# A perceiver of two layers on one core: averages 22 tiles behind the scores, weighing and spreading one step later, more one-step pauses, and the apart rows through W_k transposed

## The chip, the core and the metric

The kernel runs on one core of one Trainium2 chip. The metric is the device time of one execution in microseconds (us); smaller is better. A core has a matrix engine (TensorE, PE in the profile), a vector engine (VectorE, DVE), a scalar engine (ScalarE, ACT), a general engine (GpSimd, POOL) and a synchronising engine (SyncE, SP) that here issues most of the DMA transfers. Each runs its own stream of instructions in order; they wait for one another through semaphores.

## The reference, cut to what matters

Sixty-four latents of width 128 for each of 16 batches pass through two layers. Each layer has a cross attention over 1601 context tokens plus the latents themselves (16 heads of 64), a recurrent mixer and a feed-forward part, each behind a layer norm and with a residual:

```python
x = x + L0_xattn(ctx, layernorm(x), ...)      # 16 heads of 64, keys: 1601 context tokens and 64 latents
x = x + L0_attn(layernorm(x), ...)            # selective scan, 256 channels, 16 states
x = x + L0_ffn(layernorm(x), ...)             # small attention, then 8 experts of which 2, and a shared one
x = x + L1_xattn(ctx, layernorm(x), mask, ...)# the same attention with a mask on the context
x = x + L1_attn(layernorm(x), ...)            # convolution and scan with 4 heads of 64 by 64 states
x = x + L1_ffn(layernorm(x), ...)             # FP4-quantised gated feed-forward, 352 wide
...
logits = einsum('bhld,bhsd->bhls', q * scale, k * scale)
w = softmax(logits);  out = einsum('bhls,bhsd->bhld', w, v);  return out.reshape(B, L, INNER) @ Wo
```

All is float32.

## The kernel before

W_q and W_k are folded into one 128 by 128 matrix per head (`fold`, line 329), and W_v and W_o into another, so a head's scores are the normalised context times the folded queries, and keys and values are both just the normalised context. 1601 is not a multiple of 128: twelve tiles of 128 keys and a thirteenth that holds 64 more and the latents make 1600 + 64. The 1601st token of each batch is held **apart**: its scores `se` come from a product of its own (`apart_scores`), and its weight is `ee`.

The attention is 64 groups (layer, batch, half of the heads), each of NT = 13 key tiles, so 832 steps. A group's rows are 8 heads times 64 latents, 512 columns. `run` (line 1425) counts steps n, and `step` (1569) writes down what step n holds:

- `scores` of tile i of group g: a product of 128x512 into one of three PSUM buffers (line 662; it shows as two records), a running maximum R over the tiles on DVE (670, 672), and an eviction into a score buffer st by ACT (675, 677). The st buffers hold pairs of tiles; there are 12 of them.
- `average` (715) of the tile LAG = 21 steps earlier: st as the weights, the context tile as the moving side, into two PSUM buffers (line 725, four products, eight records a step). At the last tile `gather` (727) adds the apart token's share and makes aq.
- Of a group p whose scores are over, o = steps since: at o = 1 `maximum` (680): four transposes of R (tm), a reduction on DVE over them (692), the maximum with se, and ee; at o = 3 `spread` (700): four transposes that spread the maximum over all rows, mb, which stays in PSUM; at odd o from 3 `weigh` (707), one pair of tiles at a time: DVE subtracts mb (712), ACT takes the exponential (713). The averages of the group follow.
- Of a group whose averages are over: at o = 1 the reciprocal of the denominators, at o = 5 `turn` (776: four transposes `at`, and an ACT copy into aT, 786), at o = 8 of each second batch `output` (791).

Beside this go generators. Those in `prep` make a batch ready: `fold_qk` and `fold_vo`, `apart` (362), `latents`, `queries`, `context` (582: the loaded context's mean, line 613, variance, normalisation, and transposes kt and kt_r into kvT), `apart_scores`. Each live one is advanced by one yield a step. Those in `between` are the rest of the layers: `setup_rest`, `scan0` and `moe` (916) for four groups of batches, `scan1` (1123) and `ffn` (1372) for five; a budget per step says how many yields they get. A generator that yields HOP1, HOP, HOP3 or HOP4, `(1,)` to `(4,)`, sleeps that many steps; it is put where an engine's result is to be ready before the next instruction asks for it.

All small products go through `tp` (93), a pool of three PSUM buffers. The scheduler that builds the program may move instructions, but `behind` (1552) keeps them from moving ahead of the score step they were written in. In layer 0 there are three context buffers kv; the load of batch b is issued 48 steps ahead on SP's queue and waits for the last average of batch b-3.

`apart` before: the normalised last tokens of the 16 batches are transposed (xet, line 386, then xeT). Then, for four heads at a time, the folded matrices are transposed (line 394), copied by ACT, and multiplied by xeT (399) to give `ge`, by which `apart_scores` multiplies each pair of batches' latents. Each layer has 16 transposes and 16 products of 16 columns.

Of the kernel before, what the change touches and what calls it, by code (L numbers as in the profile page):

```python
# [32 lines left out]
F32 = mybir.dt.float32  # L33
# [9 lines left out]
P = 128  # L43
NB, L, D = 16, 64, 128
# [6 lines left out]
H, DH = 16, 64  # L51
NEG = -1.0e30
NT = G + 1
NQ = 512
LAG = 21

(LN1W, LN1B, LN2W, LN2B, NORMW, NORMB, G1, G2, YG1, YB1, YG2, YB2) = range(12)
LNOFF = 12
# [6 lines left out]
HOP1, HOP, HOP3, HOP4 = (1,), (2,), (3,), (4,)  # L65
# [8 lines left out]
CG = 2  # L74
# [5 lines left out]
class Kernel:  # L80
# [248 lines left out]
    def fold(self, lay, dst, l, r, scale):  # L329


        nc = self.nc
        for g in range(H // 4):
            if (lay, l) == (0, "WqT"):
                raw = self.raw0[g]
            else:
                raw = self.raw_pair(lay, l, r, g, nc.sync)
            if lay == 0 and l == "WvT":
                yield HOP3
            ts = [self.tp(f"{l}{lay}{g}{i}") for i in range(2)]  # L340
            for m in range(2):
                for i in range(2):
                    half = slice(i * DH, (i + 1) * DH)
                    nc.tensor.matmul(ts[i][:, m * D:(m + 1) * D], raw[0][half, m, :], raw[1][half, m, :], start=True, stop=True)
            for i in range(2):
                to = dst[:, g * 4:g * 4 + 4, :].rearrange("p (m i) d -> p i m d", i=2)[:, i]
                t = ts[i][:, :2 * D].rearrange("p (m d) -> p m d", m=2)
                if (lay, l) == (0, "WqT") and g < 2:
                    nc.scalar.activation(to, t, AF.Copy, scale=scale)
                else:  # L350
                    nc.vector.tensor_scalar_mul(to, t, scale)
            yield 0.7

    def fold_qk(self, lay):
        self.wqk = self.at.tile([P, H, D], F32, tag="wqk", name=f"wqk{lay}")
        yield from self.fold(lay, self.wqk, "WqT", "WkT", 0.125)
        self.raw0 = None

    def fold_vo(self, lay):
        self.wvo = self.at.tile([P, H, D], F32, tag="wvo", name=f"wvo{lay}")  # L360
# [1 line left out]
    def apart(self, lay):  # L362

        nc = self.nc
        w1 = self.vecs_of(lay)[0]
        xe = self.xe
        if lay == 0:
            mean, rstd, v = (self.sm([NB, 1], f"e{x}") for x in ("mean", "rstd", "var"))
            scr = self.at.tile([NB, D], F32, tag="raw", name="escr", bufs=3)
            nc.vector.tensor_reduce(mean, xe, AX.X, ALU.add)  # L370
            nc.vector.tensor_scalar_mul(mean, mean, 1.0 / D)
            nc.vector.tensor_scalar(xe, xe, mean, None, ALU.subtract)
            nc.scalar.activation(scr, xe, AF.Square)
            yield HOP1
            nc.vector.tensor_reduce(v, scr, AX.X, ALU.add)
            nc.vector.tensor_scalar(v, v, 1.0 / D, 1e-5, ALU.mult, ALU.add)
            nc.gpsimd.tensor_tensor(rstd, v, self.neghalf[:NB, :1], ALU.pow)
            yield HOP1
            nc.vector.tensor_scalar(xe, xe, rstd, None, ALU.mult)
        xw = self.at.tile([NB, D + 1], F32, tag="raw", name=f"xw{lay}", bufs=3)  # L380
        nc.vector.memset(xw[:, D:], 1.0)
        nc.vector.tensor_tensor(xw[:, :D], xe, self.vec[:NB, w1, :], ALU.mult)
        nc.sync.dma_start(out=self.xed[lay], in_=xw)
        yield HOP
        t = self.tp(f"xet{lay}")
        nc.tensor.transpose(t[:, :NB], xw[:, :D], self.ident[:NB, :NB])
        self.xeT = self.at.tile([P, NB], F32, tag="xeT", name=f"xeT{lay}")
        nc.vector.tensor_copy(self.xeT, t[:, :NB])
        yield 0.7
        self.ge = self.at.tile([P, NB, H], F32, tag="ge", name=f"ge{lay}")  # L390
        for g in range(H // 4):
            t = self.tp(f"wkq{lay}_{g}")
            for k in range(4):
                nc.tensor.transpose(t[:, k * D:(k + 1) * D], self.wqk[:, g * 4 + k, :], self.ident)
            w = self.at.tile([P, 4, D], F32, tag="raw", name=f"wkq{lay}s{g}", bufs=3)
            nc.scalar.copy(w.rearrange("p h d -> p (h d)"), t)
            o = self.tp(f"ge{lay}_{g}")
            for k in range(4):
                nc.tensor.matmul(o[:, k * NB:(k + 1) * NB], w[:, k, :], self.xeT, start=True, stop=True)
            nc.vector.tensor_copy(self.ge[:, :, g * 4:g * 4 + 4], o[:, :4 * NB].rearrange("p (h b) -> p b h", h=4))  # L400
            yield 0.7

    def apart_scores(self, lay, c):

# [511 lines left out]
    def moe(self, gr):  # L916
        nc, tc, a = self.nc, self.tc, self.a
        X = self.X[:, gr * CG:(gr + 1) * CG, :]
        with tc.tile_pool(name="mo1", bufs=1) as one, tc.tile_pool(name="mo2", bufs=2) as work:
# [8 lines left out]
            xi, nx, xT = t1([P, CG, D], "xi"), t1([P, CG, D], "nx"), t1([P, TG], "xT")  # L928
            mv, (r, rr) = self.moments(X, CG, [LN, LNRMS])
            yield 0.8  # L930
            yield HOP1
            self.scaled(nc.vector, nx, X, mv, rr, CG)
            self.scaled(nc.gpsimd, xi, X, mv, r, CG)
            yield 0.8
# [5 lines left out]
            t = self.tp("mq")  # L940
            nc.tensor.matmul(t[:, :TG], fWqT, xT, start=True, stop=True)
            nc.scalar.copy(q, t[:, :TG])
            yield 0.4
            t = self.tp("mk")
            nc.tensor.matmul(t[:, :TG], fWk4.rearrange("p r n -> p (r n)"), xT, start=True, stop=True)
            nc.scalar.copy(kT, t[:, :TG])
            t = self.tp("mv")
            for c in range(CG):
                nc.tensor.matmul(t[:, c * 32:(c + 1) * 32], xT[:, c * P:(c + 1) * P], fWkvT[:, 32:], start=True, stop=True)
# [4 lines left out]
            n = 2 * BG  # L954
            shape = [P, n, L]
            sc = t1(shape, "sc")
            m = self.sm([P, n], "mm")

            ts = [self.tp(f"ms{i}") for i in range(2)]
# [4 lines left out]
            for i in range(2):  # L964
                t3, mi, half = ts[i][:, :TG].rearrange("p (n l) -> p n l", l=L), m[:, i * BG:(i + 1) * BG], [P, BG, L]
# [5 lines left out]
            d, r = self.sm([P, n], "md"), self.sm([P, n], "mr")  # L971
# [8 lines left out]
            for j in range(2):  # L980
                t = self.tp(f"mt{j}")
# [18 lines left out]
            o = self.tp("mo")  # L1000
# [30 lines left out]
            for e in range(NE + 1):  # L1031
                w = work.tile([P, 3, FF], F32, tag="ew", name=f"ew{e}", bufs=3)
                for x, i in enumerate((1, 3, 2)):
                    nc.sync.dma_start(out=w[:, x, :], in_=a[f"e{i}T"][e])
                gu = self.tp(f"gu{e}")
                nc.tensor.matmul(gu[:, :TG], w[:, 0, :], xT, start=True, stop=True)
                nc.tensor.matmul(gu[:, TG:], w[:, 1, :], xT, start=True, stop=True)
                sg, th = (work.tile([P, TG], F32, tag=x, name=f"{x}{e}") for x in ("sg", "th"))
                nc.scalar.activation(th, gu[:, :TG], AF.Tanh, scale=0.5)
                if last:  # L1040
                    second(*last)
                    yield 0.7
                yield HOP1
                nc.vector.scalar_tensor_tensor(sg, th, 1.0, gu[:, :TG], ALU.add, ALU.mult)
                nc.vector.scalar_tensor_tensor(sg, sg, 0.5, gu[:, TG:], ALU.mult, ALU.mult)
                yield 0.9
                last = e, w, sg
# [75 lines left out]
    def scan1(self, c0, CG):  # L1123
# [5 lines left out]
        with tc.tile_pool(name="sd1", bufs=1) as one, tc.tile_pool(name="sd2", bufs=CG) as work:  # L1129
# [128 lines left out]
            for c in range(CG):  # L1258
                tok = slice(c * P, (c + 1) * P)
                for i in range(2):  # L1260
                    g = self.tp(f"gr{c}{i}")
                    part = slice(i * HD, (i + 1) * HD)
                    for k in range(2):
                        nc.tensor.matmul(g[:, k * P:(k + 1) * P], bT[part, k, tok], cT[part, k, tok], start=True, stop=True)
                    gi = gm[c].rearrange("p (k i) t -> p i k t", i=2)[:, i]
                    nc.vector.tensor_tensor(gi, g[:, :2 * P].rearrange("p (k t) -> p k t", k=2), self.row(self.upto, [P, 2, P]), ALU.mult)
                yield 0.9
            for c in range(CG):
                for lo, hi in parts:
                    sg = self.tp(f"seg{c}")  # L1270
                    for h in range(lo, hi):
                        mm = nc.tensor.matmul(sg[:, h * P:(h + 1) * P], af[c][:, h, :], self.upto, start=True, stop=True)  # L1272
                    if last and hi == NH:
                        self.fill(2, mm)
                    decay = nc.scalar.activation(af[c][:, lo:hi, :].rearrange("p h t -> p (h t)"), sg[:, lo * P:hi * P], AF.Exp)
                yield 0.1
# [292 lines left out]
    def step(self, n, ng):  # L1569
# [25 lines left out]
        for p in (g - 2, g - 1):  # L1595
            o = n - (p + 1) * NT
            if not 0 <= p < ng:
                continue
            if o == 1:
                with self.behind():  # L1600
                    self.maximum(p)
            elif o == 3:
                with self.behind():
                    self.groups[p]["mb"] = self.spread(self.groups[p]["m"], f"mb{p}")
            if o > 2 and o % 2 and (o - 3) // 2 < (NT + 1) // 2:
                self.weigh(p, (o - 3) // 2)

        d, o = divmod(n - LAG - NT, NT)
        if 0 <= d < ng:
# [69 lines left out]
```

## Time and profile before

| | us |
|---|---|
| median of 3 runs | 1976.11 |
| lowest, highest | 1975.02, 1976.44 |
| the profiled execution | 1976.84 |
| its span, first to last instruction | 1975.1 |

A profile is one execution seen by the hardware profiler. Its page gives each engine's busy time, the span in 40 slices, and the costliest groups of instructions: line, engine, operation, output and inputs, shape and count, then busy time and the mean of one in ns, then the idle time of that engine just before them and whose result ended it. A matrix product in float32 is two records. The mean granted clock of TensorE is 0.999 of full speed. A few more groups of the page:

```profile
L713 ACT ACTIVATE st<-st 128x1024 f32<-128x1024 f32 (+1 forms) x448 | 444.4, 996 | 121.6 <-DVE st L712 114.8
L712 DVE TENSOR_TENSOR st<-st,mb 128x1024 f32<-128x1024 f32 (+1 forms) x448 | 503.5, 1134 | 17.9 <-PE mb L704 17.8
L675 ACT ACTIVATE st<-s,mcol 128x512 f32<-128x512 f32 x416 | 283.4, 684 | 191.4 <-DVE R L670 167.2
L677 ACT COPY st<-s 128x512 f32<-128x512 f32 x416 | 240.0, 580 | 127.7 <-DVE R L672 117.2
```

The pair subtraction (1134 ns) and the exponential that waits for it (996 ns) come every other step; the two lines below are the eviction of the scores in the second and the first layer, which comes after the running maximum of the same tile.

### The profile page before, as it was taken

What the parts mean: (1) busy time and instruction counts of PE and PEld (TensorE: products, weight loads), DVE (VectorE), ACT (ScalarE), POOL (GpSimd) and SP (SyncE); (2) the same over time, 40 slices, a digit from 0 to 9 for tenths busy, and PEclk for the clock granted to TensorE, in tenths of its full rate; (3) what the DMA queues carried; (4) which work ended last, traced back from release to release, by engine and by line L of the source; (5) the groups of instructions that cost most, each with busy time, mean ns of one, the idle gap of its engine ahead of it and who ended that gap; (6) DMA issues with size and microseconds to landing.
All of it is one profiled execution on the core that took longest, in us unless ns stands there. A gap on an engine that the chain in (4) does not pass through costs nothing. (4 is left out here: it accounts for less than half of the span.)

```text
span 1975.1 us, 32602 instructions
## 1 busy us (share of the span) xinstructions
PE 1931.2 (98%) x11971; PEld 1478.7 (75%) x11971; DVE 1584.3 (80%) x3025; ACT 1385.2 (70%) x2642; POOL 510.4 (26%) x579
## 2 busy tenths in 40 slices
PE   8999999999999999999999999999999999999998
PEld 5777777677777767778777777777778777787786
DVE  6977776987878887876998878898786978778875
ACT  5888787887868888666776657776665665766651
POOL 5111122543123452121452203442110111101000
PEclk9999999999999999999999999999999999999999
DMA  6121112312123221221221112221120210101000
GB/s 184 49 71 47 36 54 81 85 62 70 45 66 86 76 66 53 66 79 45 69 82 54 41 35 67 71 58 54 48 68 1 58 37 20 58 18 37 23 1 22
DMA packets 144109, 110.80 MB, mean 56 GB/s; under 512 B 13762, under 2 KB 130254, under 8 KB 143950
## 3 DMA queue, kind: packets, MB, share of 16 engines
q1 hardware_dynamic: 143406, 108.46, 18.8%
q8 instruction: 95, 1.56, 0.3%
q14 instruction: 64, 0.52, 0.1%
q10 hardware_dynamic: 544, 0.26, 0.0%
HBM read 80.23 MB, written 27.41 MB: 54 GB/s over the span
## 5 line engine op out<-in xcount | busy, mean ns | idle before, releaser
L725 PEld LDWEIGHTS av<-kv,st 128*128 128x128 f32 x6656 | 870.0, 192 | 375.7 <-issue 356.3
L725 PE MATMUL av<-kv,st 128*128 128x129 f32 x6656 | 882.2, 275 | 4.1 <-DVE aq L734 4.0
L662 PE MATMUL s<-qT,kvT 128*128 128x512 f32 x1664 | 857.7, 598 | 9.1 <-ACT st L677 6.6
L713 ACT ACTIVATE st<-st 128x1024 f32<-128x1024 f32 (+1 forms) x448 | 444.4, 996 | 121.6 <-DVE st L712 114.8
L712 DVE TENSOR_TENSOR st<-st,mb 128x1024 f32<-128x1024 f32 (+1 forms) x448 | 503.5, 1134 | 17.9 <-PE mb L704 17.8
L675 ACT ACTIVATE st<-s,mcol 128x512 f32<-128x512 f32 x416 | 283.4, 684 | 191.4 <-DVE R L670 167.2
L677 ACT COPY st<-s 128x512 f32<-128x512 f32 x416 | 240.0, 580 | 127.7 <-DVE R L672 117.2
L670 DVE SCALAR_TENSOR_TENSOR R<-s,mcol,R 128x512 f32<-128x512 f32 x352 | 261.9, 744 | 44.0 <-PE s L662 42.8
L672 DVE TENSOR_TENSOR R<-s,R 128x512 f32<-128x512 f32 x352 | 240.7, 684 | 64.0 <-PE s L662 62.6
L662 PEld LDWEIGHTS s<-qT,kvT 128*128 128x128 f32 x1664 | 254.4, 191 | 24.7 <-ACT st L677 11.5
L578 POOL TENSOR_TENSOR kv<-kv,vec 128x384 f32<-128x384 f32 (+1 forms) x128 | 130.8, 1042 | 146.9 <-PE kt L637 35.2
L774 POOL TENSOR_TENSOR aq<-aq,rd 128x512 f32<-128x512 f32 x63 | 74.4, 1181 | 340.8 <-DVE rd L773 329.3
L878 POOL TENSOR_TENSOR db<-sc_u,bb 128x512 f32<-128x512 f32 x64 | 83.6, 1309 | 123.5 <-DVE h L889 63.9
L895 POOL TENSOR_TENSOR sc_y<-sc_y,h 128x512 f32<-128x512 f32 x60 | 80.9, 1349 | 117.4 <-DVE h L894 100.9
L889 DVE TENSOR_TENSOR_SCAN h<-da,db 128x512 f32<-128x512 f32 x64 | 91.4, 1429 | 0.5 <-ACT da L877 0.5
L628 ACT ACTIVATE kv<-kv,coff,crstd 128x128 f32<-128x128 f32 x182 | 76.2, 490 | 6.0 <-POOL coff L625 6.0
L734 DVE SCALAR_TENSOR_TENSOR aq<-xeb,ee,av 128x129 f32<-128x129 f32 x252 | 76.2, 341 | 0.0
L619 ACT ACTIVATE scr<-kv,cmean 128x128 f32<-128x128 f32 x182 | 72.6, 399 | 2.8 <-DVE cmean L615 0.6
L135 POOL TENSOR_TENSOR crstd<-cvar,neghalf 128x13 f32<-128x13 f32 x14 | 34.2, 2440 | 138.5 <-DVE cvar L623 138.1
L455 PE MATMUL q<-xnT,wqk 128*128 128x128 f32 x512 | 68.4, 277 | 0.0
L455 PEld LDWEIGHTS q<-xnT,wqk 128*128 128x128 f32 x512 | 62.6, 192 | 2.9 <-issue 1.4
L672 DVE TENSOR_TENSOR R<-s,st 128x512 f32<-128x512 f32 x32 | 22.0, 687 | 52.0 <-PE s L662 43.4
(412 smaller groups left out, 1939.1 us busy)
## 6 DMA issues: line engine op xcount, KB each, us to landing
bb<-bcd SPq DMA_DIRECT2D x64, 256.0 KB, 4.5
xh<-kv SPq DMA_DIRECT2D x16, 832.0 KB, 4.7
kv<-xh SPq DMA_DIRECT2D x16, 832.0 KB, 5.5
kvT<-xhT SPq DMA_DIRECT2D x16, 800.0 KB, 4.6
xhT<-kvT SPq DMA_DIRECT2D x15, 800.0 KB, 3.4
kv<-in_ctx_dram SPq DMA_DIRECT2D x15, 768.0 KB, 5.4
ew<-in_e1T_dram SPq DMA_DIRECT2D x36, 64.0 KB, 1.8
ew<-in_e3T_dram SPq DMA_DIRECT2D x36, 64.0 KB, 2.0
```

Of the source, the lines that this page charges most:

```text
L455: nc.tensor.matmul(t[:, k * P:(k + 1) * P], self.wqk[:, g * 4 + k, :], xnT, start=True, stop=True)
L578: nc.gpsimd.tensor_tensor(kv[:, lo:hi, :D], kv[:, lo:hi, :D], self.row(self.vec[:, w1, :], [P, hi - lo, D]), ALU.mult)
L662: mm = nc.tensor.matmul(s, self.kv_of[lay, b][1][:, i * P:(i + 1) * P], q, start=True, stop=True)
L670: mx = nc.vector.scalar_tensor_tensor(R, s, mc, last, ALU.add, ALU.max)
L672: mx = nc.vector.tensor_tensor(R, s, last, ALU.max)
L675: ev = nc.scalar.activation(st, s, AF.Identity, bias=mc)
L677: ev = nc.scalar.copy(st, s)
L712: nc.vector.tensor_tensor(st, st, self.row(mb, [P, n, NQ]), ALU.subtract)
L713: nc.scalar.activation(st, st, AF.Exp)
L725: nc.tensor.matmul(grp["av", j][:, k, :], st, self.kv_of[lay, b][0][:, i, :], start=(i == 0 and k == 0), stop=(i == NT - 1 and k == 1))
L878: nc.gpsimd.tensor_tensor(db, u, self.row(bb[:, 0, s % 2, :], both), ALU.mult)
L889: nc.vector.tensor_tensor_scan(flat(h), flat(da), flat(db), 0.0, ALU.mult, ALU.add)
```

## The change

Averages come 22 steps behind the scores instead of 21. `spread` goes from o = 3 to o = 4, `weigh` from odd to even o; `maximum` keeps o = 1. What is counted from LAG (`turn`, `output`, the start of the `between` generators) moves with it. `moe`, `scan1` and `fold` get HOPs at places named in the diff; in an expert, the second product of the expert before (`second`) goes behind the HOP. `apart` no longer transposes the folded matrices. It transposes the raw W_k, four blocks of 128 at a time (one ACT copy), multiplies by xeT (four products of 16 columns, kx, scaled on DVE), and multiplies kx by the raw W_q in half-height products (64 rows, one head each) to give ge. In layer 0 the raw matrices are those that `fold_qk` loaded, which are kept until then, and the transposes of W_k stand ahead of xet; in layer 1 they are loaded anew, four more DMA transfers.

```diff
--- before.py
+++ after.py
@@ -52,7 +52,7 @@
 NEG = -1.0e30
 NT = G + 1
 NQ = 512
-LAG = 21
+LAG = 22
 
 (LN1W, LN1B, LN2W, LN2B, NORMW, NORMB, G1, G2, YG1, YB1, YG2, YB2) = range(12)
 LNOFF = 12
@@ -335,8 +335,9 @@
                 raw = self.raw0[g]
             else:
                 raw = self.raw_pair(lay, l, r, g, nc.sync)
-            if lay == 0 and l == "WvT":
-                yield HOP3
+            if (lay, l) != (0, "WqT"):
+
+                yield HOP4 if lay == 0 else HOP
             ts = [self.tp(f"{l}{lay}{g}{i}") for i in range(2)]
             for m in range(2):
                 for i in range(2):
@@ -354,7 +355,6 @@
     def fold_qk(self, lay):
         self.wqk = self.at.tile([P, H, D], F32, tag="wqk", name=f"wqk{lay}")
         yield from self.fold(lay, self.wqk, "WqT", "WkT", 0.125)
-        self.raw0 = None
 
     def fold_vo(self, lay):
         self.wvo = self.at.tile([P, H, D], F32, tag="wvo", name=f"wvo{lay}")
@@ -362,6 +362,27 @@
     def apart(self, lay):
 
         nc = self.nc
+
+        def turned(n):
+
+            if lay == 0:
+                raw = [[self.raw0[2 * n + m // 2][x][:, m % 2, :] for m in range(4)] for x in range(2)]
+            else:
+                raw = []
+                for x in ("WqT", "WkT"):
+                    t = self.at.tile([P, 4, D], F32, tag="raw", name=f"g{x}{n}", bufs=3)
+                    nc.sync.dma_start(out=t, in_=self.a[f"L1{x}"].rearrange("(m p) d -> p m d", p=P)[:, 4 * n:4 * n + 4, :])
+                    raw.append([t[:, m, :] for m in range(4)])
+                yield HOP3
+            t = self.tp(f"wk{lay}{n}")
+            for m in range(4):
+                nc.tensor.transpose(t[:, m * P:(m + 1) * P], raw[1][m], self.ident)
+            w = self.at.tile([P, 4, D], F32, tag="raw", name=f"wk{lay}s{n}", bufs=3)
+            nc.scalar.copy(w.rearrange("p m j -> p (m j)"), t)
+            wk.append((w, raw[0]))
+            yield 0.7
+
+        wk = []
         w1 = self.vecs_of(lay)[0]
         xe = self.xe
         if lay == 0:
@@ -381,24 +402,39 @@
         nc.vector.memset(xw[:, D:], 1.0)
         nc.vector.tensor_tensor(xw[:, :D], xe, self.vec[:NB, w1, :], ALU.mult)
         nc.sync.dma_start(out=self.xed[lay], in_=xw)
-        yield HOP
+        if lay:
+            yield HOP
+        else:
+            for n in range(2):
+                yield from turned(n)
+            yield HOP1
         t = self.tp(f"xet{lay}")
         nc.tensor.transpose(t[:, :NB], xw[:, :D], self.ident[:NB, :NB])
         self.xeT = self.at.tile([P, NB], F32, tag="xeT", name=f"xeT{lay}")
         nc.vector.tensor_copy(self.xeT, t[:, :NB])
         yield 0.7
         self.ge = self.at.tile([P, NB, H], F32, tag="ge", name=f"ge{lay}")
-        for g in range(H // 4):
-            t = self.tp(f"wkq{lay}_{g}")
-            for k in range(4):
-                nc.tensor.transpose(t[:, k * D:(k + 1) * D], self.wqk[:, g * 4 + k, :], self.ident)
-            w = self.at.tile([P, 4, D], F32, tag="raw", name=f"wkq{lay}s{g}", bufs=3)
-            nc.scalar.copy(w.rearrange("p h d -> p (h d)"), t)
-            o = self.tp(f"ge{lay}_{g}")
-            for k in range(4):
-                nc.tensor.matmul(o[:, k * NB:(k + 1) * NB], w[:, k, :], self.xeT, start=True, stop=True)
-            nc.vector.tensor_copy(self.ge[:, :, g * 4:g * 4 + 4], o[:, :4 * NB].rearrange("p (h b) -> p b h", h=4))
+        for n in range(2):
+            if lay:
+                yield from turned(n)
+            w, wq = wk[n]
+            t = self.tp(f"kx{lay}{n}")
+            for m in range(4):
+                nc.tensor.matmul(t[:, m * NB:(m + 1) * NB], w[:, m, :], self.xeT, start=True, stop=True)
+            kx = self.sm([P, 4, NB], "kx")
+            nc.vector.tensor_scalar_mul(kx.rearrange("p m b -> p (m b)"), t[:, :4 * NB], 0.125)
+            yield 0.5
+
+            ts = [self.tp(f"ge{lay}{n}{i}") for i in range(2)]
+            for m in range(4):
+                for i in range(2):
+                    half = slice(i * DH, (i + 1) * DH)
+                    nc.tensor.matmul(ts[i][:, m * NB:(m + 1) * NB], wq[m][half], kx[half, m, :], start=True, stop=True)
+            for i in range(2):
+                to = self.ge[:, :, 8 * n:8 * n + 8].rearrange("p b (m i) -> p i b m", i=2)[:, i]
+                nc.vector.tensor_copy(to, ts[i][:, :4 * NB].rearrange("p (m b) -> p b m", m=4))
             yield 0.7
+        self.raw0 = None
 
     def apart_scores(self, lay, c):
 
@@ -928,7 +964,7 @@
             xi, nx, xT = t1([P, CG, D], "xi"), t1([P, CG, D], "nx"), t1([P, TG], "xT")
             mv, (r, rr) = self.moments(X, CG, [LN, LNRMS])
             yield 0.8
-            yield HOP1
+            yield HOP
             self.scaled(nc.vector, nx, X, mv, rr, CG)
             self.scaled(nc.gpsimd, xi, X, mv, r, CG)
             yield 0.8
@@ -941,9 +977,12 @@
             nc.tensor.matmul(t[:, :TG], fWqT, xT, start=True, stop=True)
             nc.scalar.copy(q, t[:, :TG])
             yield 0.4
+            yield HOP1
             t = self.tp("mk")
             nc.tensor.matmul(t[:, :TG], fWk4.rearrange("p r n -> p (r n)"), xT, start=True, stop=True)
             nc.scalar.copy(kT, t[:, :TG])
+            yield 0.3
+            yield HOP1
             t = self.tp("mv")
             for c in range(CG):
                 nc.tensor.matmul(t[:, c * 32:(c + 1) * 32], xT[:, c * P:(c + 1) * P], fWkvT[:, 32:], start=True, stop=True)
@@ -1037,10 +1076,10 @@
                 nc.tensor.matmul(gu[:, TG:], w[:, 1, :], xT, start=True, stop=True)
                 sg, th = (work.tile([P, TG], F32, tag=x, name=f"{x}{e}") for x in ("sg", "th"))
                 nc.scalar.activation(th, gu[:, :TG], AF.Tanh, scale=0.5)
+                yield HOP1
                 if last:
                     second(*last)
                     yield 0.7
-                yield HOP1
                 nc.vector.scalar_tensor_tensor(sg, th, 1.0, gu[:, :TG], ALU.add, ALU.mult)
                 nc.vector.scalar_tensor_tensor(sg, sg, 0.5, gu[:, TG:], ALU.mult, ALU.mult)
                 yield 0.9
@@ -1265,6 +1304,8 @@
                     gi = gm[c].rearrange("p (k i) t -> p i k t", i=2)[:, i]
                     nc.vector.tensor_tensor(gi, g[:, :2 * P].rearrange("p (k t) -> p k t", k=2), self.row(self.upto, [P, 2, P]), ALU.mult)
                 yield 0.9
+                if c + 1 < CG:
+                    yield HOP1
             for c in range(CG):
                 for lo, hi in parts:
                     sg = self.tp(f"seg{c}")
@@ -1599,11 +1640,11 @@
             if o == 1:
                 with self.behind():
                     self.maximum(p)
-            elif o == 3:
+            elif o == 4:
                 with self.behind():
                     self.groups[p]["mb"] = self.spread(self.groups[p]["m"], f"mb{p}")
-            if o > 2 and o % 2 and (o - 3) // 2 < (NT + 1) // 2:
-                self.weigh(p, (o - 3) // 2)
+            if o > 3 and o % 2 == 0 and (o - 4) // 2 < (NT + 1) // 2:
+                self.weigh(p, (o - 4) // 2)
 
         d, o = divmod(n - LAG - NT, NT)
         if 0 <= d < ng:
```

## The prediction

> **What bounds the kernel now.** I read the page's busy times first, then its costliest groups, the table by windows, and the waits of PE.
>
> ```profile
> PE 1931.2 (98%) x11971; PEld 1478.7 (75%) x11971; DVE 1584.3 (80%) x3025; ACT 1385.2 (70%) x2642; POOL 510.4 (26%) x579
> ...
> L725 PE MATMUL av<-kv,st 128*128 128x129 f32 x6656 | 882.2, 275 | 4.1 <-DVE aq L734 4.0
> L662 PE MATMUL s<-qT,kvT 128*128 128x512 f32 x1664 | 857.7, 598 | 9.1 <-ACT st L677 6.6
> ```
>
> The averages (882) and the scores (858) are 88% of the span and nothing here changes them. They stand in 832 steps of about 2.37 us, each with 1.03 us of scores and 1.06 us of averages.
>
> ```profile
> 0.00:60.00 60.00, 54.76 (x300) 36.23 (x301) 42.92 (x146) 35.84 (x77) 29.05 (x54) 1.00 0.59 172
> 60.00:500.00 440.00, 432.85 (x2665) 327.19 (x2663) 349.11 (x598) 361.88 (x795) 126.52 (x129) 1.00 0.20 60
> 500.00:1000.00 500.00, 486.90 (x3004) 371.26 (x3003) 401.25 (x756) 375.42 (x790) 155.25 (x162) 1.00 0.23 66
> 1000.00:1500.00 500.00, 493.28 (x3075) 378.43 (x3074) 422.75 (x782) 337.92 (x546) 140.74 (x149) 1.00 0.19 55
> 1500.00:1900.00 400.00, 397.05 (x2477) 307.84 (x2476) 324.81 (x625) 252.75 (x394) 52.09 (x74) 1.00 0.11 31
> 1900.00:1975.00 75.00, 66.39 (x462) 57.75 (x460) 43.45 (x123) 21.41 (x43) 6.78 (x12) 1.00 0.05 15
> ```
>
> Columns: the stretch, then busy us of PE, PEld, DVE, ACT, POOL, then the clock. PE is the fullest engine in every stretch. It lacks 5, 7, 13, 7, 3 and 9 us of the stretches: 44 us in all is what can be won by removing waits. DVE and ACT are at 80% in the middle, so a wait can be pushed elsewhere there. Who holds PE up (total, times, longest):
>
> ```profile
> PE s L662 <- ACT st L677: 6.6, 11, 1.4
> PE av L725 <- DVE aq L734: 4.0, 5, 1.3
> PE me L1022 <- DVE sg L1045: 2.9, 3, 1.8
> PE mb L704 <- DVE tm L695: 2.5, 4, 1.4
> ...
> PE mb L704 <- DVE m L693: 2.0, 2, 1.5
> PE gr L1264 <- DVE gm L1266: 1.8, 1, 1.8
> PE mot L177 <- DVE mo_nx L162: 1.6, 2, 1.3
> ...
> PE mv L949 <- ACT mo_q L942: 1.3, 1, 1.3
> PE xet L386 <- DVE fmv L595: 1.2, 1, 1.2
> ```
>
> These are few waits, about 1 us each. Each is an instruction issued one or two steps after its producer, which was late that time. The two largest rows (s, av) are not what the edits aim at.
>
> [...] By the trace, PE's starts follow each other at the usual distance (0.112 us for an average's record, 0.43 for a score's) but for some 41 us of gaps. [...]
>
> **The change, part by part.**
>
> **Lag 22, and mb and the weighing one step later.** `maximum` stays at o=1, `spread` goes from o=3 to o=4, `weigh` from odd to even o, and averages follow, so weigh-to-average keeps its distance. In the instruction order 204 of the 256 mb transposes stood two steps behind their maximum and 40 one step; afterwards 216 stand three and 32 two. By the gaps of the trace those one step behind cost about 0.48 us per group, those two behind 0.02. So the mb rows (2.5 + 2.0 + 0.5 + 0.2 by DVE and ACT, 5.2) should fall to 0.5: **-4.7**. The amount of work is unchanged. One tile's averages (1.06 us) go from the start, where PE is 91% busy, to after the last score, where averages run alone: 0 if the start has no other work for the hole, +1.06 if it does not fill; I take 0, as the start's holes are 5 us already.
>
> **Turn and maximum in one step.** Averages 22 behind move `turn` by one step while `maximum` stays, so both now fall in the same step of every group, with one weighing. There are three small PSUM slots: mb holds one for twelve of thirteen steps, tm and at take the others. tm is released by the DVE reduction (0.69 us a piece, then 0.16 each for three small ones), which may stand behind a subtraction of 1.13 us; at is released by the ACT copy (0.69). What is issued third waits: in the order, instructions that follow their releaser within the same step go from 6 to 17 in layer 0 (kt_r behind df, bc behind aT), and from 7 to 2 in layer 1. The mean gap of such an instruction in this trace is 0.12 us, for aT's 0.24, at most the copy's 0.69. So 11 x 0.12..0.24 = 1.3 to 2.6; **+2**, bounds 0 (other slots come free first) and +6. What queues behind the waiting transpose on PE is the whole stream.
>
> **HOPs in moe, scan and folds.** No instruction is added; one step is put between producer and use. me behind sg goes from six uses in the same step to one: 2.9 to 0.9, **-2.0**. gr and seg, **-1.7** of 2.0. mot 1.6 to 0.1, **-1.5**. mv (1.3 + 0.7), **-1.7**. Fold matrices waiting for raw DMAs and X (1.4 + 0.6 + 0.5), **-1.5**. xet gets W_k's transposes ahead of it, **-1.2**. In exchange moe's groups end some three experts later, in steps with more scan work; that has no row, I count 0, and +2 at most (three experts' me and gu waits at 0.7).
>
> Sum of the waits aimed at: -4.7 - 2.0 - 1.7 - 1.5 - 1.7 - 1.5 - 1.2 = **-14.3**. Those in the full stretches of DVE (703, 1308, 1417 us) will be partly taken by the next score's eviction; the rows s and av show that. I count three quarters, **-10.7** (bounds -14.3 and -4, the latter if only classes' mean gaps are saved).
>
> **The kv reload.** In layer 0 the buffer of batch b comes from b-3 and is free one step later. The mean's reduction (1.08 us) stands first on DVE behind the load, and DVE waits 9.2 us for it now. In the order that reduction itself moves one step later for eleven of thirteen batches; two keep their place and can lose up to a step's 2.4 us, which DVE's 20% of slack takes mostly: **+1** (0 to +4). Behind it on DVE stand the running maximum and, through it, the score's PSUM buffer.
>
> **The apart rows.** Per layer, before: 16 transposes and 16 products of 16 columns (32 records). In the trace that is 32 x 0.11 + 64 x 0.112 = 3.5 + 7.2 = 10.7 us for both layers. After: 8 transposes, 8 full products, and 16 half-height ones (32 records): 1.75 + 3.6 + half-height blocks. [...] The trace's own half-height blocks (L344) run pairs 105 ns apart, but lose about 0.2 us on entering and again on leaving, 1.23 us for a block of sixteen records; four blocks are 4.9. So 10.3 against 10.7, **-0.4**; by the rule -1.8; +2.6 if every pair broke. Four ACT copies of 0.58 us less and four small DVE copies more lie beside PE. The four added DMA loads on SP are issued three steps ahead of use, in steps 396 to 416 where the DMA share is 0.2: 0. In layer 0, ge now ends two steps ahead of the eviction that needs its buffer; that cover gone would cost 0.7.
>
> Sum: -10.7 + 2 + 1 - 0.4 + 0 = **-8.1**. The profiled execution took 1976.84 us (1975.1 span and 1.7 outside); it becomes 1968.7. The median of the runs shown stands 0.7 lower (1976.11), so I predict **1968.0**.
>
> **Rivals.**
>
> *Waits move, not vanish.* [...] Against: layer 1's waits are isolated, with PE 99% busy after 1500. Savings by class means only, -4, then +2 +1 - 0.4 = -1.4: median **1974.7**.
>
> *Slower: tm and at contend for two PSUM slots.* In 62 groups, the transposes that come next in that step wait for the DVE reduction behind a 1.13 us subtraction, or the aT copy. Neither was in that step before. At 0.3 us a group it is 18.6, with the gains of 10.7 +1 -0.4: +8.5, **1984.6**. It decides from 0.16 us a group (10.1 / 62), where it eats the gains. Against: only 17 instructions stand directly behind their releaser in layer 0, and 2 in layer 1.
>
> *The apart rows buy nothing or ge disturbs the start.* +2.6 and 0.7 instead of -0.4: **1971.7**. It is inside the first case.
>
> *The change doesn't do what it says.* The order shows mb and the HOPs moved; excluded but for the kv reductions.
>
> **How the numbers follow.** A measurement of this kernel tells 0.2%, 4 us, from no change: 1972.2 to 1980.1. The forecast with its sizes (1961 to 1972): 0.60. Waits only move (1972 to 1979): 0.18. The contention: 0.22, from which 0.20 lies above 1980. Faster 0.61, same 0.17, slower 0.22. The lower end is -14.3 with +0, 1961; the upper end reaches into the contention, 1982; 0.2 are left out.
>
> **What would show it.** Right: rows of mb, mv and mot below 0.5 each and me below 1, PE's waits near 32 us, PE busy unchanged within 1 us. The contention would be seen as new rows of kt, kt_r, bc, tm or at waiting for aT or df, of 5 us or more together. The moved waits would be seen as s behind st above 10. DVE's wait for kv above 15 us would show the reload late. The forecast is wrong if ge's half-height blocks are above 2 us each, or if a cluster at step 389 (moe's end) grows by several us.

## The result, and the profile after

The changed kernel takes 1983.84 us (1980.03 to 1985.22) against 1976.11 (1975.02 to 1977.98) before: ratio 1.0033, 95% interval 1.0023 to 1.0044. It is slower by a little, where 1968.0 was forecast. Its profiled execution is the quickest of its five runs, 1980.03 us with a span of 1978.3; beside before's profiled 1976.84 it shows +3.2 of the +7.7.

The page after, busy times and the two large groups:

```profile
PE 1929.3 (98%) x11987; PEld 1477.3 (75%) x11987; DVE 1587.5 (80%) x3029; ACT 1382.5 (70%) x2638; POOL 513.1 (26%) x579
...
L761 PE MATMUL av<-kv,st 128*128 128x129 f32 x6656 | 880.0, 275 | 3.7 <-DVE aq L770 3.3
L698 PE MATMUL s<-qT,kvT 128*128 128x512 f32 x1664 | 860.7, 600 | 13.4 <-ACT st L713 11.1
```

PE's busy time fell by 1.9 us, but the idle time ahead of the scores rose from 9.1 to 13.4. The same stretches as before (the last is 4 us longer; columns as there):

```profile
60.00:500.00 440.00, 432.12 (x2642) 326.09 (x2642) 347.75 (x590) 360.19 (x793) 125.77 (x129) 1.00 0.20 60
500.00:1000.00 500.00, 485.64 (x3008) 370.42 (x3007) 399.83 (x756) 370.42 (x783) 151.75 (x157) 1.00 0.23 66
1000.00:1500.00 500.00, 492.20 (x3072) 376.73 (x3071) 423.29 (x772) 340.50 (x546) 144.97 (x150) 1.00 0.20 57
1500.00:1900.00 400.00, 393.48 (x2469) 306.47 (x2468) 324.57 (x638) 250.13 (x394) 54.01 (x76) 1.00 0.11 31
```

From 1500 to 1900 us PE lacked 3 us before and lacks 6.5 now. What PE waits for (total, times, longest):

```profile
PE s L698 <- ACT st L713: 11.1, 16, 2.5
PE av L761 <- DVE aq L770: 3.3, 5, 1.9
PE fft L177 <- DVE ff_xi L1386: 2.9, 2, 2.3
PE tm L722 <- DVE R L706: 2.4, 1, 2.4
PE sdt L177 <- DVE sd_xi L162: 2.1, 2, 1.8
PE xnt L177 <- DVE xn L162: 2.1, 2, 1.7
PE gu L1075 <- DMA ew<-in_e1T_dram: 1.8, 1, 1.8
...
PE xnt L177 <- DVE X L1064: 1.5, 1, 1.5
...
PE me L1061 <- DVE sg L1084: 1.2, 1, 1.2
```

Most waits that were aimed at are gone or small: mb (5.2), mot, mv, xet and the gr of 1.8 have no row, me fell from 2.9 to 1.2. The fold's wait for its raw load stayed (WvT behind rawWvT: 1.4 before, 1.6 now). Yet all rows together went from 39.8 to 45.1 us. That is +5.3; less 1.9 of busy time it is +3.4, close to the +3.2 of the span. The new rows are longer single waits, elsewhere: eight of 1.7 to 2.5 us, where before had two (1.8 each).

The granted clock also fell, behind a stretch in which PE was half busy. Three windows of 3.41 us in a row, in the kernel after:

```profile
358.69:362.11 3.42, 1.70 (x13) 1.31 (x12) 3.42 (x8) 1.97 (x6) 1.52 (x3) 1.00 0.02 5
362.11:365.52 3.41, 2.83 (x7) 1.79 (x8) 1.03 (x3) 3.41 (x9) 2.44 (x2) 0.50 0.29 105
365.52:368.93 3.41, 3.41 (x27) 2.88 (x26) 3.41 (x4) 3.41 (x8) 1.28 (x1) 1.00 0.33 90
```

PE is busy 1.70 of 3.42 us, and in the next 3.41 us its clock is 0.50. Such a stretch is called a dip below. Over the 192 runs of the kernel before that stood beside the experiments, one thousandth of the mean clock goes with 1.33 us; a dip of 3.41 us at half is 0.0009 of the span. The mean clock of these runs is 0.9987. The median after stands 3.8 us above its own profiled execution, with a clock 0.0014 lower (0.9976 in the mean of the five, 0.999 in the profiled one): by that slope some 1.9 us of it are dips, an estimate, and the other 2 no profile here shows. The +3.2 of the two profiles is not a matter of dips: each has one (at 1609.60 us before, at 362.11 after) and another that begins in its last microseconds (1974.83, 1976.61).

### The profile page after: what moved, and what is told of

It is laid out like the page before. It is cut to its first block, busy times and chain, and to the rows that moved or that the text cites. A ratio compares the mean times of both kernels' runs of the same rounds, so it can differ in the third digit from the quotient of the medians.

```text
span 1978.3 us, 32633 instructions
## 1 busy us (share of the span) xinstructions
PE 1929.3 (98%) x11987; PEld 1477.3 (75%) x11987; DVE 1587.5 (80%) x3029; ACT 1382.5 (70%) x2638; POOL 513.1 (26%) x579
## 4 chain that ended last, share of the span: by engine, by line
PE 51%; DVE 9%; issue 3%; ACT 3%; DMA 2%; POOL 1%; POOLq 0%; SPq 0%; DVEq 0%; ACTq 0%
PE av L761 20%; PE s L698 18%; DVE R L706 3%; DVE st L748 2%; PE q L491 2%; PE o L833 2%; PE at L821 1%; PE tm L722 1%; PE mb L740 1%; ACT st L749 1%; PE me L1061 1%; PE sb L1262 1%; PE gu L1075 1%; DVE R L708 1%; PE gu L1076 1%
## 5 line engine op out<-in xcount | busy, mean ns | idle before, releaser
L698 PE MATMUL s<-qT,kvT 128*128 128x512 f32 x1664 | 860.7, 600 | 13.4 <-ACT st L713 11.1
L706 DVE SCALAR_TENSOR_TENSOR R<-s,mcol,R 128x512 f32<-128x512 f32 x352 | 262.4, 745 | 44.6 <-PE s L698 42.1
L682 ACT ACTIVATE kvT<-kvT,vcol 128x768 f32<-128x768 f32 (+1 forms) x62 | 58.3, 960 | 16.2 <-DMA xhT<-kvT 16.2
```

Source lines behind the costliest of these rows:

```text
L698: mm = nc.tensor.matmul(s, self.kv_of[lay, b][1][:, i * P:(i + 1) * P], q, start=True, stop=True)
L706: mx = nc.vector.scalar_tensor_tensor(R, s, mc, last, ALU.add, ALU.max)
```

## The experiments

All times are medians, and each ratio is against runs of the kernel before in the same rounds on the same chip (1976.7, 1976.7, 1975.3, 1976.5 and 1976.5 us in the five sets); "clock" is the mean over a kernel's runs. Nothing computed is left out in any of them.

**First set: the parts, and turn.** e1 takes the hunks of the lag, spread and weigh alone, e2 those of moe and scan1, e3 those of fold and apart. e4 is the changed kernel with

```diff
-                elif o == 5:
+                elif o == 4:
                     self.turn(d)
```

> The kernel before with only the lag of 22 and spread and weigh one step later (maximum stays at o=1). Theory A (waits move: what the pauses take from one place comes back as other waits, and long gaps bring clock dips): within 3 us of 1976, mb rows below 0.5 us. Theory B (turn and maximum share a step and the PSUM slots): +6 to +9 us, with waits of tm, kt or at on aT or df. Theory C (the pauses in moe and scan push moe's end late, so latents, expert weights and tails wait): -3 to -5 us, since the mb waits (5.2 us) go and nothing else is touched.

Measured: 1980.56, ratio 1.002 (1.0011 to 1.0028), clock 0.9967. mb has no row, s behind st (the first layer's eviction) is 10.3 instead of 6.6.

> The kernel before with only the pauses in moe and scan1 (and the second product behind its pause). Theory A: within 3 us of 1976, me, mot, mv, gr rows gone and as much in others. Theory B: -3 to -6 us, for seven us of waits are aimed at and turn stays apart from maximum. Theory C: +3 to +6 us, with new waits of xnt for X, gu for its expert weights, or fft and sdt.

Measured: 1981.57, 1.0023 (1.0014 to 1.0032), clock 0.9951. mot, mv and gr are gone; mb behind tm is 5.5 (2.5 before), s behind both evictions is 13.2 (8.2 before), with one wait of 4.4 at 723 us and one of 4.0 at 1678 us.

> The kernel before with only the apart rows through W_k transposed and the pauses in fold. All of A, B and C: within 2 us of 1976 (PE's own work about -0.4 us, by the profile after -2 us of PE busy; fold and xet waits -1 to -2). If it is above 1979, a fourth cause holds: the longer life of the raw matrices disturbs the start or the change of layers.

Measured: 1972.86, 0.9979 (0.9972 to 0.9987). It is better than expected; the waits fell by 3.0, of which xet is 1.2. The fold's wait for its raw load is still 1.4.

> The changed kernel with turn at o=4 instead of o=5, so that it falls in the step before maximum, as in the kernel before. Theory B: 4 to 8 us faster than the changed kernel, about 1976 to 1979. Theories A and C: within 2 us of the changed kernel, 1982 to 1986.

Measured: 1985.24, 1.0043 (1.003 to 1.0056), no quicker than the changed kernel (1.0033). Theory B, turn and maximum contending in one step, falls. The lag part and the pauses each cost, apart gains.

**Second set: is it any shift of the fill work?** e5 is the kernel before with all `between` stages one step later, e6 is e1 with them at the old steps, e7 and e8 split e2:

```diff
 e5   done = lambda lay, b: start(lay, b) + LAG + 11       (was + 10; setup_rest at LAG + 1)
 e6   done = lambda lay, b: start(lay, b) + LAG + 9        (LAG is 22; setup_rest at LAG - 1)
 e7   only second() behind HOP1 in the experts
 e8   only HOP1 between the halves of gr
```

> The kernel before with nothing but every between generator started one step later (the lag stays 21, weigh and spread stay, no pause is added). Theory A2 (the place of the fill work against the attention's fixed steps decides, and any shift of it makes other instructions stand at the head of an in-order queue while late): 1978 to 1982, with other long gaps (2 us and more) near 700 to 780, 1250 and 1600 to 1680 us and a clock of 0.996 to 0.998. Theory L (the lag of 22 itself costs, by the weighing's new step or the buffers): within 1 us of before, since neither is touched.

Measured: 1975.71, 0.9994 (0.9985 to 1.0002). A uniform step costs nothing. DVE's wait for the context load rose to 13.7 us (9.2 before) at no cost, so a later reload is no cause either.

> The lag change alone (22, spread and weigh a step later), but the between generators start at the steps of the kernel before. Theory A2: the loss of the lag change (1980.6) is gone, 1973 to 1977, since the mb waits of 5.2 us go and the rest stands as before. Theory L: 1980 to 1982 again.

Measured: 1980.13, 1.0018 (1.0011 to 1.0024): the loss of the lag part stays. A2 in this form, any shift costs, falls twice.

> The kernel before with only the second product of an expert put behind its pause (no pause is added, no stage moves). Theory A2: -1 to -3 us (the me waits of 2.9 go), since nothing shifts. A theory that the pauses of moe are harmless and the swap costs (the product's weights are freed later and the expert's DMA comes late): +2 to +4 us, with gu waiting for its weights.

Measured: 1974.17, 0.9986 (0.998 to 0.9993).

> The kernel before with only the pause between the two halves of gr in scan1, five times in layer 1. Theory A2: +1 to +4 us, though gr's own wait (1.8) goes: all stages after it in layer 1 stand one step later, and long waits of sdt, fft or s appear at 1250, 1600 or 1680 us. A theory that each pause is worth the wait it removes: -1.5 to -2 us, no other row changed.

Measured: 1973.93, 0.9989 (0.9983 to 0.9996). Both edits gain, so the loss of e2 lies in moe's other pauses. The wait of gr is 0.9 (1.8 before, where the dip at 1609.60 us begins behind it), and the clock is 0.9991 in the mean of e8's runs, 0.9986 in that of before's beside them.

**Third set: finer parts.** e9 has only the pauses ahead of `scaled` and between q, kT and v; e10 only LAG = 22; e11 only spread and weigh; e12 is e3, e7 and e8 together.

> The kernel before with only the pauses in moe that put steps between products and what they wait for: two steps instead of one ahead of scaled, one step each behind q and behind kT. The swap in the experts and gr are left as before. If the parts of the pauses add up (all together +4.9, the swap -2.5, gr -2.8), this is +8 to +11 us, about 1986. If the loss of all together comes from moe's and scan1's pauses acting on each other, it is -3 to +3 us.

Measured: 1980.91, 1.0028 (1.0017 to 1.0039), clock 0.9953.

> The kernel before with only the lag at 22: spread stays at o=3, weigh at odd o, so the weighing is one step further from its averages. Theory K (averages later: the context buffers come free later, gather and turn move): +2 to +4 us, s waiting for st in layer 0 above 9 us, DVE's wait for the context above 12 us. Theory W (the weighing's new step is what collides): within 1.5 us of before.

Measured: 1977.31, 1.001 (1.0004 to 1.0017).

> The kernel before with only spread at o=4 and weigh at even o, the lag at 21. Theory W: +2 to +4 us, s waiting for st above 9 us. Theory K: -1 to -4 us, the mb waits of 5.2 gone and nothing else moved, though weigh to average is a step shorter.

Measured: 1973.24, 0.9992 (0.9984 to 1.0). The mb rows are gone, but s behind st is 12.2 us instead of 6.6 and all rows sum to 39.8, as before. That profile is the slowest of the 13 runs (1976.8); the median gains 2.1, at the edge of its interval. Lag and weigh apart give +2.0 and -2.1, together +3.9.

> The kernel before with the three parts that were faster alone: the apart rows with fold's pauses (-3.8), the swap in the experts (-2.5) and gr's pause (-2.8). If each removes its own waits and they don't act on each other: -7 to -10 us, 1967 to 1970. If what is removed at one place comes back at another: -3 to -5 us, 1972 to 1974.

Measured: 1967.52, 0.9964 (0.9951 to 0.9976), clock 0.9994: quicker than both kernels, and the best of all. Its profile has no PE wait above 1.5 us in one piece, and its clock is 1.000 (0.999 in before's profile).

**Fourth set: how do moe's pauses cost?** The stages in `between` run one after another. In the program's order scan1's first product (sdt) stands in step 645 before and in 657 in e9: three steps more for each of four moe stages. The second of the five scan1 stages moves from 689 to 701; the third stands in 762 in both. e13 is the kernel before with nearly as much delay (sdt in 658) and no pause at any product; e14 is e9 with a budget that brings the stages back to within a step:

```diff
 e13
             second(*last)
             yield 0.7
+            yield HOP4
 e14
-            between.append((done(0, (gr + 1) * BG), 0.75, self.moe(gr)))
+            between.append((done(0, (gr + 1) * BG), 0.85, self.moe(gr)))
```

> The kernel before with four idle steps at the end of each of the four moe stages (the stages after it start 3, 6, 9 and 13 steps later, as with moe's pauses; no product is moved away from what it waits for). Theory S (the longer chain lands on worse places): +4 to +7 us, with long waits of s at 720 and 1678 us, sdt at 1600 and mb at 1253 us. Theory P (the pauses themselves cost, in moe): within 2 us of before.

Measured: 1980.27, 1.0022 (1.0011 to 1.0034), clock 0.9961.

> moe's pauses (as the run with these alone), but moe's budget per step is 0.85 instead of 0.75, so that the next stages start at the steps of the kernel before (scan0 at 265, 392, 519, scan1 at 646 instead of 645). Theory S: -1 to -4 us against before (mot and mv waits of 3.6 us go). Theory P: +4 to +6 us as with the pauses alone.

Measured: 1973.06, 0.9986 (0.998 to 0.9993). Theory S (the longer chain puts stages in worse places) holds on both sides. One thing stays mixed: the larger budget also packs moe's own instructions closer, and it was not run alone. PE's waits in e9, then in e13:

```profile
PE s L662 <- ACT st L677: 10.5, 12, 4.3
PE mb L704 <- DVE tm L695: 6.4, 6, 2.4
PE s L662 <- ACT st L675: 4.7, 2, 3.8
PE sdt L177 <- DVE sd_xi L162: 3.1, 2, 2.7
```

```profile
PE s L662 <- ACT st L677: 8.2, 9, 4.3
PE mb L704 <- DVE tm L695: 5.8, 5, 2.4
PE s L662 <- ACT st L675: 4.3, 3, 3.0
```

The delay alone makes three of the same waits (4.3 at 722 us, 3.0 at 1676, 2.4 at 1255); that of sdt it does not (0.4). How the wait of 4.3 comes about is in e13's timeline (start, us, engine, line; in brackets the idle time before and who ended it):

```profile
715.22 1.28 POOL L878 TENSOR_TENSOR db<-sc_u,bb 128x512 f32<-128x512 f32 x1 [2.63 <-DVE cvar L623]
...
716.45 2.44 POOL L135 TENSOR_TENSOR crstd<-cvar,neghalf 128x13 f32<-128x13 f32 x1
...
718.97 0.41 POOL L625 TENSOR_TENSOR coff<-cmean,crstd 128x13 f32<-128x13 f32 x1
...
719.42 2.03 ACT L628 ACTIVATE kv<-kv,coff,crstd 128x128 f32<-128x128 f32 x5 [3.04 <-POOL coff L625]
...
721.35 0.56 ACT L677 COPY st<-s 128x512 f32<-128x512 f32 x1
...
721.97 1.48 PE L662 MATMUL s<-qT,kvT 128*128 128x512 f32 x2 [4.33 <-ACT st L677]
```

POOL runs scan0's db (1.28) ahead of the context's inverse root (2.44). ACT has the context's normalisation next in its queue, so it sits idle for 3.04 us; then it does five pieces (2.03), and only then the eviction for which PE has waited 4.33 us. In the kernel before the root stands ahead of db, and PE's longest wait there is 1.4:

```profile
713.43 2.44 POOL L135 TENSOR_TENSOR crstd<-cvar,neghalf 128x13 f32<-128x13 f32 x1
...
716.12 1.27 POOL L878 TENSOR_TENSOR db<-sc_u,bb 128x512 f32<-128x512 f32 x1
716.20 2.03 ACT L628 ACTIVATE kv<-kv,coff,crstd 128x128 f32<-128x128 f32 x5 [2.39 <-POOL coff L625]
...
718.75 1.12 PE L662 MATMUL s<-qT,kvT 128*128 128x512 f32 x2 [1.45 <-ACT st L677]
```

In e13 PE was busy 0.64 of the 3.41 us up to 722.61, and the clock in the next 3.41 us is 0.50.

> The whole change without moe's pauses ahead of scaled and between q, kT and v (lag, spread, weigh, apart, fold, swap and gr as changed). If the parts add up (3.9 - 3.8 - 2.5 - 2.8): -5 us, 1970 to 1973. If the lag's loss grows with the rest: 1975 to 1979.

e15 is the whole change without moe's pauses ahead of `scaled` and between q, kT and v. Measured: 1976.55, 1.0001 (0.9993 to 1.0009): level with before. Against e12 it has only the lag, the spread and the weighing's step more, and they take all of e12's gain of 7.8. s behind st is 11.0 in its profile (6.5 in e12), and all rows sum to 40.8 (35.1).

> The three parts that were faster alone (apart with fold, swap, gr; -7.8 together), with spread at o=4 and weigh at even o in the second layer only, lag 21. If the weighing's step only collides in layer 0 (s behind st, behind the context's work on ACT): 1.5 to 3 us faster than the three parts, 1964 to 1966. If it collides as well in layer 1: no gain, 1967 to 1969.

e16 is e12 with spread and weigh's first step at `3 + layer`. Measured: 1971.78, 0.9977 (0.997 to 0.9984): no gain but a loss against e12, beyond both forecasts. In layer 1 a turn (at) now waits 2.5 us for POOL's aq, as in e11.

**Fifth set: the whole change with its stages put back.** e17 is the changed kernel with 0.85 for 0.75 as in e14; sdt stands in step 647. e18 is e12 and e14 together.

> The whole change, with moe's budget per step 0.85 instead of 0.75, so that its stages start one step later than in the kernel before (as the lag has it) and not 4, 7, 10 and 13 later. If the longer chain is what the whole change loses by: 1973 to 1977 (without moe's pauses it was level with before). If the lag's loss and the pauses add up whatever the place of the stages: 1982 to 1986 as the whole change.

Measured: 1971.11, 0.9972 (0.9961 to 0.9983). One number in a budget turns the change from 7.7 us slower to 5.4 quicker, though its clock (0.9979 in the mean) is still below before's. Its page and its first waits:

```profile
PE 1931.3 (98%) x11987; PEld 1479.7 (75%) x11987; DVE 1585.3 (81%) x3029; ACT 1384.5 (70%) x2638; POOL 514.8 (26%) x579
```

```profile
PE s L698 <- ACT st L713: 9.1, 13, 2.5
PE av L761 <- DVE aq L770: 2.7, 4, 1.4
PE av L761 <- ACT st L749: 2.3, 1, 2.3
```

The tm wait of 2.4, the fft of 2.3 and the sdt of 1.8 are not there; all rows sum to 34.0 us (45.1 in the changed kernel). The s wait of 2.5 at 722 us stays: it is also in e1 and e15, and in the changed kernel the root stands ahead of db, so it belongs to the lag part.

How the tm wait arose in the changed kernel is in its timeline, the normalisation for the second ffn stage:

```profile
1669.00 0.18 DVE L145 BATCH_NORM_AGGREGATE mv<-bs 128x2 f32<-128x6 f32 x1
...
1670.53 1.18 POOL L614 TENSOR_TENSOR kv<-kv,vec 128x512 f32<-128x512 f32 x1 [5.58 <-DMA kv<-xh]
...
1671.80 0.19 POOL L155 TENSOR_SCALAR var<-mv 128x2 f32<-128x2 f32 x1
1672.07 1.04 POOL L810 TENSOR_TENSOR aq<-aq,rd 128x512 f32<-128x512 f32 x1
...
1673.06 0.70 POOL L135 TENSOR_TENSOR rstd<-var,neghalf 128x2 f32<-128x2 f32 x1
...
1673.80 1.88 DVE L162 TENSOR_SCALAR ff_xi<-X,mv,rstd 128x128 f32<-128x128 f32 x2 [3.03 <-POOL rstd L135]
...
1676.73 0.73 DVE L706 SCALAR_TENSOR_TENSOR R<-s,mcol,R 128x512 f32<-128x512 f32 x1
...
1677.52 0.65 PE L722 MATMUL tm<-ident,R 128*128 128x128 f32 x4 [2.43 <-DVE R L706]
```

The statistics mv are ready at 1669.2, but POOL waits for a DMA until 1670.5, does kv (1.18) and aq (1.04) ahead of rstd, and DVE stands idle for 3.03 us with the running maximum behind. In e17 the same stage comes some twelve steps earlier; var follows mv at once, and DVE waits 1.09:

```profile
1641.34 0.60 DVE L162 TENSOR_SCALAR ff_xi<-X,mv,rstd 128x128 f32<-128x128 f32 x2 [1.09 <-POOL rstd L135]
```

In e13, with the delay alone, DVE waits 4.96 us for this rstd, ahead of PE's wait of 3.0 at 1676.

> All parts but the lag and the weighing's step: apart with fold, the swap, gr, and moe's pauses with the budget 0.85, lag 21. If the parts' gains add up (-7.8 for three parts, -3.4 for the pauses at the old steps): -9 to -11 us, 1965 to 1967.5. If the pauses' gain is used up by the others: -6 to -8, 1968 to 1970.

Measured: 1971.91, 0.9976 (0.9966 to 0.9985): the two gains do not add, and e12 stays the best.

## Why the prediction was wrong, step by step

**The step that failed** is the sentence "In exchange moe's groups end some three experts later, in steps with more scan work; that has no row, I count 0, and +2 at most". The delay was seen, but taken for a matter of moe alone. It lengthens a chain of stages, by 3, 6, 9 and 12 steps, so all stages in it up to the second ffn meet the attention's fixed work elsewhere. Alone it measured +3.8 (e13), with moe's pauses +5.6 (e9). In the whole change moe's pauses cost 7.6 us (from e15 to the changed kernel), and the larger budget brings back 12.7 (to 1971.11 in e17). If the pauses keep their own gain there (3.4 in e14), the delay costs some 11 to 13 us in the whole change, an estimate from these three.

**A second term failed as badly**: the lag with spread and weigh. By the forecast's own terms it is -0.5 (three quarters of mb's -4.7, +2 for turn, +1 for the reload). The forecast's -8.1 and the measured +7.7, each as a difference to before, divide like this:

| added in this order | forecast | measured | run |
|---|---|---|---|
| apart, folds, second, gr | -5.2 | -7.8 | e12 |
| lag, spread, weigh | -0.5 | +7.9 | e15 |
| moe's pauses ahead of `scaled`, between q, kT, v | -2.4 | +7.6 | the changed kernel |

The sizes depend on the order, for the parts act on each other: the lag with spread and weigh is +3.9 alone (e1), and level on top of moe's pauses with the larger budget (e17 against e18).

**What bounds the kernel** was read rightly: PE's waits and busy time add up to the span within 4.1 us, before and after, and PEld's busy share stayed at 75% while the time moved both ways (1983.84 after, 1967.52 in e12). Not in the sum was the clock, 0.50 for 3.41 us behind the windows from 1606.19 us before, 358.69 after and 719.20 in e13.

**The pauses' own worth** was sized rightly, where the stages stayed: second -2.5 (forecast -2.0 for me), gr -2.8 (-1.7), mot and mv -3.4 (-3.2; e14, with the larger budget). **Apart** with xet and folds gave -3.8 (-3.1 forecast), but not by the forecast's items: the fold's wait for its raw load stayed. The half-height blocks last 1.0 us from the first start to the next product, 1.23 was taken; the wait for xet is gone. The -1.8 beside the forecast's -0.4 for these blocks is shown by no run: four of 1.0 us are 4.0 in all.

**mb**: the wait fell as forecast, the time did not. Forecast -4.7, measured -2.1 alone (e11, hardly clear of noise), and a loss of some 3 when added in layer 1 to the three other parts (e16). In their place PE waited for evictions (e11) and for POOL's aq (e11, e16).

**The lag**: counted 0 for the averages' later end, +2 for turn and +1 for the reload; measured +2.0 alone (e10), so the size was near, but neither of the two was found as its cause (e4, e5). With the weighing's step it is +3.9. Why these two act on each other, and why they cost 7.9 on top of e12 and nothing on top of e18, stays open; the steps of the `between` stages don't explain it (e6).

**The sum itself.** Three quarters of the aimed waits were to stay won, as one share for all. e12 keeps 7.8 of the 9.1 us that its three parts gained alone, e18 4.6 of the 11.2 that e12 and e14 gained. There is no fixed share.

**The rivals.** The apart rows were worth their place (e3). The contention of tm and at named almost the measured time, 1984.6, by luck and for a wrong reason: turn put back changed nothing (e4), and no rows of kt or bc behind aT appeared. "Waits move" came nearest: its sign, s behind st above 10, was met (11.1). But it did not say what pushes the evictions, nor that it could exceed what was removed. The kv reload is no cause: DVE's wait for it rose from 9.2 to 10.8 us in the changed kernel, and to 13.7 in e5 without a loss.

## What to carry to other kernels

Where fill work goes through a serial chain beside a fixed pipeline, a pause may gain at its place and still lose, since it moves the stages behind it: count the steps to where the chain catches up, and give the budget back before judging the pause. Look for the first instruction in each in-order queue that is late (here a root on POOL, of 2.44 us behind 1.28 of db in e13 and of 0.70 behind 1.18 of kv and 1.04 of aq in the changed kernel, then what waits for it on ACT or DVE, then the eviction or the maximum): PE's stalls of 4.33 and 2.43 us began there. Judge parts alone and together: gains here did not add up, and the sign of one part changed with the others.

## What the runs showed of the hardware that was not expected

Three windows were followed by 3.41 us at a clock of 0.50 although PE had not been idle all through them: PE was busy 1.62 of 3.41 us in the kernel before (from 1606.19, with its gr wait of 1.8), 1.70 of 3.42 in the changed kernel (from 358.69) and 0.64 of 3.41 in e13 (from 719.20, with the s wait of 4.33). Half-busy windows without a dip behind them were measured too. With the profiles of before and after laid out in windows of 3.413 us that end where the dip begins, and without the first 60 us and the last 12, eight windows were busy between 0.46 and 0.50, and none less. The dip followed on two of them (0.48 before, 0.50 after) and none on the other six (1415.04 before; 720.51, 1191.55, 1338.32, 1601.15 and 1679.65 after). What tells the two kinds apart is not shown. In the kernel before, the gr wait of 1.8 us and 3.41 us at 0.50 thus stand one behind the other. The twelve runs of e1, at 0.9967, average nearly four times 0.0009 below full clock.

In the rows around 1674 us above, the two ff_xi instructions took 1.88 us where e17's took 0.60. POOL ran three kv instructions in that time:

```profile
1673.73 2.73 POOL L614 TENSOR_TENSOR kv<-kv,vec 128x384 f32<-128x384 f32 x3
```

In the profiles of before and after, DVE instructions of this line (L162, 128x128) took 0.33 to 0.35 us in the 56 cases without POOL beside them. The four that had such a kv instruction beside them for most of their time took 0.60 (at 148.15 before) and 0.73, 0.98 and 0.98 us (at 147.24, 1673.80 and 1674.69 after). Beside other POOL work they took 0.33 to 1.29. The running maximum (L706) took 0.74 us beside such a kv (17 cases) and 0.75 without POOL (267) in the changed kernel. So the stage that moved also met POOL work here, and its own two DVE instructions took 1.88 us.
